# Seven-product form for the q, k and v projections of layer 2 and the q projection of layer 3 in a four-layer attention stack, with MLP weight sums made by tile pairs

## Chip, cores, metric

One core of a Trainium2 chip runs the whole program. The metric is the device time of one execution in microseconds (us); lower is better. Engines: PE (TensorE: matmuls into PSUM), PEld (its weight loads), DVE (VectorE), ACT (ScalarE), POOL (GpSimd), SP (SyncE, which issues the DMAs).

## What is computed

Four layers in a chain on x of shape (4 batches, 512 tokens, 512 features), all in float32, with a context of (4, 64, 512). Cut to what the change touches:

```python
# layer 0: two cross-attentions over the context, then gelu(h @ w_fc1 + b) @ w_fc2 + b, F = 2048
# layer 1: cross-attention with weights that are folded into the context
# layer 2, 16 heads of 32; keys and values from the 64 context rows AND from the 512 rows of x
q  = x @ q_w + q_b                                  # (512 x 512) @ (512 x 512) for each batch
kv = concat([ctx, x]) @ kv_w + kv_b                 # k and v, each 512 x 512 for each batch
x  = gelu(rmsnorm(softmax(q k^T) v @ out_w + out_b + x) @ mlp_w1 + b1) @ mlp_w2 + b2 + x
# layer 3, 16 heads; keys and values from the context alone
q  = layer_norm(x) @ q_w + q_b
x  = x + softmax(q k_ctx^T) v_ctx @ cproj_w + cproj_b
x  = x + gelu(layer_norm(x) @ fc_w + fc_b) @ proj_w + proj_b
```

## The kernel before

**Layout.** After layer 0's attention the activations lie transposed: `xT[b][c]` is a tile of 128 features by 512 tokens, four (c) for each batch b. A projection of one batch is thus 4 output tiles, each 4 matmuls of 128x128 weights by 128x512 tokens summed in a PSUM bank (`mm4`, L634). `projected` (L1140) does it for layer 3's q, `sliced` (L1148) for layer 2's q and k with weights loaded as slices of 128 columns, and for v the roles are swapped: x is the stationary side and `L2_wv` the moving one (L1246 to L1253). Each result leaves PSUM with a bias added (L493 on DVE, L496 and L492 on ACT, L1252 on DVE for v).

**MLP.** `mlp` (L910) already takes two batches at once by Strassen's scheme in Winograd's form: a 2x2 block product made with 7 block products instead of 8. The blocks are halves of the features by halves of the output columns on the weight side, and halves of the features by the two batches on the other. `stationary_sums` (L868) loads one quarter of a weight matrix (512 x 512) as four blocks of 256 KB and makes four sums of 128x512 elements; `moving_sums` (L886) makes eight sums for the two batches; `seven` (L899, its matmuls are L907) makes the products, 2 matmuls of 512 columns each. The sums of weights and activations go through `added` (L864), whose one instruction (L866) may run on DVE or on POOL.

**Order of the work.** Nothing is issued in the order in which it is written. `Plan` records every operation with an estimated cost for each engine it may run on, then `order` simulates the five engines and writes out one fixed sequence for each engine's queue. The highest-ranked ready operation on an engine goes first; it may run ahead of the oldest unfinished one by `AHEAD` = 150 us of PE work (loads: 60 us), and only if its buffers fit. SBUF is one arena of 24 blocks of 2080 floats in each partition, given out in halves of halves (a 512-float tile takes 520, a quarter block). Work that is further ahead than 15 us has to leave 4 whole blocks free. Where an attempt finds no room, `order` starts again with the look-ahead cut to 20 us around that place. PSUM is 8 banks.

**Streams.** The rank comes from `beside` (L275): several streams are interleaved by the share of their PE work that is done, so that MLP matmuls fill the waits of an attention. In time: layer 0's attention; MLP 0 of batches 0 and 1 beside layer 1's weights; MLP 0 of batches 2, 3 beside layers 1 and 2's attention of batches 0, 1; MLP 2 of 0, 1 beside layers 1 and 2's attention of 2, 3; MLP 2 of 2, 3 beside layer 3's attention of 0, 1; MLP 3 of 0, 1 beside layer 3's attention of 2, 3; MLP 3 of 2, 3 alone.

**Layer 2's attention** (`l2_attention`, L1239) then takes four heads at a time: scores of context (L1265) and of x (L1294, four matmuls on 32 rows each), maximum on DVE (L1305, L1307), exponential on ACT (L1317), transposes of the weights on PE (L1351, L1357), copies out (L487 on ACT, L488 on DVE), the product with v (L1381). Layer 3's scores are L1164, 4 matmuls of 256 columns at a time, its layer norms use L1182 to L1229.

Of the kernel before, what the change touches and what calls it, by code (L numbers as in the profile page):

```python
# [76 lines left out]
class View:  # L77
# [5 lines left out]
    def __init__(self, buf, key=None, path=()):  # L83
        self.buf, self.key, self.path = buf, key, path
# [112 lines left out]
class Plan:  # L197
# [8 lines left out]
    SHARED_DVE, SHARED_POOL = 0.45, 0.15  # L206
    PATIENCE = 3.0

    def __init__(self, sbuf, ahead, ahead_load, reserve):
        self.reserve = reserve  # L210
        self.sbuf = Memory(BLOCK, sbuf)
        self.psum = Memory(1024, 4)
        self.ahead, self.ahead_load = ahead, ahead_load
        self.ops = []
        self.pos = 0.0

    def sb(self, n):
# [56 lines left out]

    def beside(self, *streams):  # L275


        first, at = len(self.ops), self.pos
        spans = []
        for stream in streams:  # L280
            i, pos = len(self.ops), self.pos
            stream()
            length = max(self.pos - pos, 1e-9)
            spans += [((op.pos - pos) / length, op) for op in self.ops[i:]]
        spans.sort(key=lambda s: s[0])
        pos = at
        for i, (_, op) in enumerate(spans):
            op.n, op.pos = first + i, pos
            self.ops[first + i] = op
            pos += op.engines.get("PE", 0.0)  # L290

    def order(self):


        waits = [op.wait for op in self.ops]
        left = {id(b): (b, b.left) for op in self.ops for b in op.uses}
        narrow = []
        while True:
            for op, n in zip(self.ops, waits):
                op.wait = n  # L300
            for b, n in left.values():
                b.left, b.at = n, None
            self.sbuf.reset()
            self.psum.reset()
            out, at = self.attempt(narrow)
            if out:
                return out
            width = 100 + 100 * sum(lo <= at <= hi for lo, hi in narrow)
            if width > 1500:
                raise RuntimeError(f"no room at {at}: {self.sbuf.free}, {self.psum.free}")  # L310
            narrow.append((at - width, at + 50))
# [247 lines left out]
def stack(nc, const, sbuf, psum, a, out):  # L559
# [30 lines left out]
        mterm3.rearrange("p b s -> p (b s)"), mk_b, 0.0, LOWEST, ALU.is_equal, ALU.mult  # L590
    )

    pl = Plan(BLOCKS, AHEAD, AHEAD_LOAD, RESERVE)
    sb, ps = pl.sb, pl.ps

    def col(name, i=None):
# [4 lines left out]
    def pe(us):  # L601
        return pl.op(PE=us)
# [24 lines left out]
    def chunks(w):  # L627

        return w.rearrange("(c p) n -> p c n", p=P)
# [235 lines left out]
        with pl.op(DVE=t_dve(n), POOL=t_pool(n)) as o:  # L865
            o.tensor_tensor(out, x, y, op)  # L866

    def stationary_sums(src):  # L868

        a11, a12, a21, a22 = (  # L870
            loaded(chunks(src)[:, 2 * r : 2 * r + 2, m * 256 : m * 256 + 256], 2, 256).v(2, 256)
            for m in range(2)
            for r in range(2)
        )
        sums = [sb(512).v(2, 256) for _ in range(4)]
        added(sums[0], a21, a22, ALU.add, 512)
        added(sums[2], a11, a21, ALU.subtract, 512)
        added(sums[1], sums[0], a11, ALU.subtract, 512)
        added(sums[3], a12, sums[1], ALU.subtract, 512)

        def part(view):
            return lambda c, m: view[:, c, m * P : (m + 1) * P]

        return [part(v) for v in (a11, a12, a22, *sums)]

    def moving_sums(h0, h1):  # L886

# [8 lines left out]
            ops.append((b11, b21, b22, t4, t1, t2, t3))  # L896
        return [(lambda c, i=i: ops[c][i]) for i in range(7)]

    def seven(A, T, m):  # L899

        a11, a12, a22, s1, s2, s3, s4 = A
        b11, b21, b22, t4, t1, t2, t3 = T
        for lhs, rhs in ((a11, b11), (s2, t2), (s3, t3), (s1, t1), (a12, b21), (a22, t4), (s4, b22)):
            p = ps()
            with pe(2 * MM[512]) as o:
                for c in range(2):
                    o.matmul(p.v(), lhs(c, m), rhs(c), start=(c == 0), stop=(c == 1))  # L907
            yield p

    def mlp(layer, pair, hT, func, table, b1, b2):  # L910
# [21 lines left out]
            return t  # L932

        for q in range(F // 512):
            A = stationary_sums(a[f"L{layer}_w1"][:, q * 512 : (q + 1) * 512])
            g0, g1 = [None] * NC, [None] * NC

            def gelu(g, f, src):
                g[f] = sb(S)
                with act(S, table) as o:  # L940
                    o.activation(g[f].v(), src.v(), func, bias=col(b1, q * NC + f))  # L941

            for m in range(2):
                made = seven(A, T, m)
                u1 = moved(next(made))
                u2 = plus(next(made), u1)
                u3 = plus(next(made), u2)
                p5 = moved(next(made))
                gelu(g1, 2 + m, sum_of(p5, u3))
                u4 = sum_of(p5, u2)  # L950
                gelu(g0, m, plus(next(made), u1))
                gelu(g0, 2 + m, plus(next(made), u3))
                gelu(g1, m, plus(next(made), u4))
            A = stationary_sums(a[f"L{layer}_w2"][q * 512 : (q + 1) * 512, :])
            G = moving_sums(g0, g1)
            for m in range(2):
                made = seven(A, G, m)
                for r in kept[m]:
                    p = next(made)
                    if q == 0:  # L960
                        with either(S) as o:
                            o.move(r.v(), p.v())
                    else:
                        with dve(S) as o:
                            o.tensor_tensor(r.v(), p.v(), r.v(), ALU.add)  # L965
                for r, d in ((x0[m], m), (x0[2 + m], 2 + m), (x1[m], m)):
                    p = next(made)
                    with dve(S) as o:
                        if q == 0:
                            o.scalar_tensor_tensor(r.v(), p.v(), col(b2, d), r.v(), ALU.add, ALU.add)  # L970
                        else:
                            o.tensor_tensor(r.v(), p.v(), r.v(), ALU.add)
                if q == last:
                    p1, p6, p7, p5 = (r.v() for r in kept[m])
                    x11, x21, x12, x22 = x0[m].v(), x0[2 + m].v(), x1[m].v(), x1[2 + m].v()
                    added(x11, x11, p1, ALU.add, S)
                    added(p6, p6, p1, ALU.add, S)
                    added(p7, p7, p6, ALU.add, S)
                    added(x21, x21, p7, ALU.add, S)
                    added(p6, p6, p5, ALU.add, S)  # L980
                    added(x12, x12, p6, ALU.add, S)
                    added(p7, p7, p5, ALU.add, S)
                    with pl.op(DVE=t_dve(S)) as o:
                        o.scalar_tensor_tensor(x22, p7, col(b2, 2 + m), x22, ALU.add, ALU.add)
# [160 lines left out]
            o.shift(t.v(), p.v(), col(name, d))  # L1145
        return t

    def sliced(name, src, bias, d):  # L1148

        p = ps()  # L1150
        w = loaded(chunks(a[name][:, d * P : (d + 1) * P]), NC, P)
        with pe(4 * MM[512]) as o:
            mm4(o, p.v(), lambda c: w.v(NC, P)[:, c, :], lambda c: src[c].v())
        t = sb(S)
        with either(S) as o:
            o.shift(t.v(), p.v(), col(bias, d))
        return t

    def context_scores(q, kd, t, mterm, b, qs):

# [73 lines left out]

    def l2_context():
        row = load_row("L2_v_b")
        shared2.update(row=row, ckT=context_keys(2, "L2_k_b"), cv=context_values(2, row))

    def l2_attention(b):  # L1239
        qs = 1.0 / DH  # L1240
        row, ckT, cv = shared2["row"], shared2["ckT"], shared2["cv"][b]
        xb = xT[b]
        kd = diagonal_keys(ckT, b)
        wv = loaded(chunks(a["L2_wv"]), NC, 512)
        v = []
        for t in range(NT):  # L1246
            p = ps()
            with pe(4 * MM[512]) as o:
                mm4(o, p.v(), lambda c: xb[c][:, t * P : (t + 1) * P], lambda c: wv.v(NC, 512)[:, c, :])
            n = sb(D)  # L1250
            with dve(D) as o:
                o.tensor_tensor(n.v(), p.v(), row.v(), ALU.add)  # L1252
            v.append(n)  # L1253
        oT = []
        for g in range(NC):
            q = sliced("L2_wq", xb, "L2_xattn_q_b", g)
            k = sliced("L2_wk", xb, "L2_k_b", g)

            sc, mc = [], []
            for i in range(NT // 2):  # L1260
# [23 lines left out]
            for half in range(2):  # L1284
# [102 lines left out]
                            )  # L1387
                with dve(2 * P) as o:
                    o.tensor_tensor(made[:, half * 2 * P : (half + 1) * 2 * P].k(half), p[:, : 2 * P], rT.v(), ALU.mult)
            oT.append(made)  # L1390
        wo = loaded(chunks(a["L2_wo"]), NC, 512)
        y = []
        for d in range(NC):
# [17 lines left out]

    def l3_context():
        row = load_row("L3_xattn_v_b")
        shared3.update(ckT=context_keys(3, "L3_xattn_k_b"), cv=context_values(3, row))

    def l3_attention(b):
# [1 line left out]
        cv = shared3["cv"][b]  # L1418
        h = layer_norm(xT[b], "L3_xattn_ln1_w", "L3_xattn_ln1_b")
        kd = diagonal_keys(shared3["ckT"], b)  # L1420
        wq = loaded(chunks(a["L3_wq"]), NC, 512)
        q = [projected(wq, h, "L3_xattn_q_b", d) for d in range(NC)]
        prT = [sb(4 * S) for _ in range(2)]
        for t in range(NT):
            sc = context_scores(q, kd, t, mterm3, b, qs)
# [129 lines left out]

BLOCK, BLOCKS = 8 * KW, 24
AHEAD, AHEAD_LOAD, RESERVE = 150.0, 60.0, 4


# [54 lines left out]
```

## Time and profile before

| what | value |
|---|---|
| median of 3 runs | 2855.93 us (2852.36 to 2856.58) |
| profiled execution | 2855.12 us, of which the span from first to last instruction is 2853.2 us |
| mean granted TensorE clock | 0.994 |
| PE busy in the span | 2772.7 us, 10540 instructions |
| DVE / ACT / POOL busy | 1817.4 / 814.2 / 916.0 us |
| DMA | 129.62 MB, mean 45 GB/s |

How to read it: a float32 matmul stands in the trace as two records of its line (1344 matmuls of `seven` are 2688 records), so counts of records are twice the matmuls; transposes have one record. A record of a PE group has a duration from entry to end, and the next one enters before it has ended, so the pace is read from the chain of waits or a timeline, not from the mean duration. "Idle before" is the time for which an engine had nothing running ahead of an instruction, and the name after it is what came last. The windows view gives busy microseconds of each engine in a stretch of the span.

### The profile page before, as it was taken

Reading aid. Unit: us, or ns where it says so; the run is one execution under the profiler, and the core shown is the slowest. Engines: PE = TensorE matmul, PEld = TensorE weight load, DVE = VectorE, ACT = ScalarE, POOL = GpSimd, SP = SyncE. Lnnn points to the kernel's source line nnn. Section 1 sums busy time; section 2 is a strip of 40 time slices with the busy share of each in tenths; the row PEclk is TensorE's granted clock in tenths of the full one; section 3 lists DMA queues with packets and bytes.
Section 4 is the critical chain, followed back from the end, with each engine's and each line's share of the span. In section 5 each row is a group of like instructions: output and inputs, shape, how many; then the busy total and the mean of one; then the engine's idle time right before and its main releaser. Section 6 shows DMA issues by size and latency. Waiting matters only on the chain. (4 is left out here: it accounts for less than half of the span.)

```text
span 2853.2 us, 29411 instructions
## 1 busy us (share of the span) xinstructions
PE 2772.7 (97%) x10540; PEld 1499.2 (53%) x10540; DVE 1817.4 (64%) x3102; ACT 814.2 (29%) x1471; POOL 916.0 (32%) x859
## 2 busy tenths in 40 slices
PE   8999999999999999998999999999999998999999
PEld 6676666666654444544555555444444444444444
DVE  5645656555745567756677577576775677567665
ACT  1210212102311114634362355245432323232211
POOL 2710216202521241212124112311543456344531
PEclk9999999999999999999999999999999999999999
DMA  5022020120102110010012001101101120111110
GB/s 163 30 60 67 26 67 23 56 63 1 60 30 77 60 44 19 27 45 30 23 38 71 8 25 44 59 27 41 45 30 44 45 74 15 44 45 60 59 45 30
DMA packets 131025, 129.62 MB, mean 45 GB/s; under 512 B 6800, under 2 KB 105744, under 8 KB 130880
## 3 DMA queue, kind: packets, MB, share of 16 engines
q1 hardware_dynamic: 130512, 127.43, 14.1%
q8 instruction: 84, 1.38, 0.2%
q14 instruction: 61, 0.50, 0.1%
q0 software_dynamic: 80, 0.16, 0.0%
q10 hardware_dynamic: 288, 0.15, 0.0%
HBM read 123.52 MB, written 4.19 MB: 45 GB/s over the span
## 5 line engine op out<-in xcount | busy, mean ns | idle before, releaser
L907 PE MATMUL banks<-arena 128*128 128x512 f32 x2688 | 1210.1, 596 | 19.5 <-DVE arena L866 6.7
L634 PE MATMUL banks<-arena 128*128 128x260 f32 (+3 forms) x2480 | 825.9, 486 | 2.7 <-ACT arena L496 1.1
L907 PEld LDWEIGHTS banks<-arena 128*128 128x128 f32 x2688 | 497.6, 190 | 615.4 <-issue 528.3
L866 POOL TENSOR_TENSOR arena<-arena 128x512 f32<-128x512 f32 x304 | 437.1, 1445 | 678.1 <-DVE arena L488 173.3
L634 PEld LDWEIGHTS banks<-arena 128*128 128x128 f32 x2480 | 454.6, 189 | 329.3 <-issue 287.2
L488 DVE COPY arena<-banks 128x512 f32<-128x512 f32 (+3 forms) x526 | 305.4, 586 | 180.9 <-PE banks L907 66.3
L487 ACT COPY arena<-banks 128x512 f32<-128x512 f32 (+2 forms) x366 | 190.8, 542 | 710.5 <-PE banks L907 191.1
L866 DVE TENSOR_TENSOR arena<-arena 128x512 f32<-128x512 f32 x308 | 302.7, 989 | 69.2 <-ACT arena L941 26.3
L941 ACT ACTIVATE arena<-arena,cols 128x512 f32<-128x512 f32 x192 | 137.8, 721 | 448.8 <-DVE arena L866 221.4
L926 DVE TENSOR_TENSOR arena<-banks,arena 128x512 f32<-128x512 f32 x240 | 163.9, 686 | 131.1 <-PE banks L907 120.7
L1317 ACT ACTIVATE arena<-banks,arena 128x512 f32<-128x512 f32 x256 | 174.5, 686 | 115.1 <-DVE arena L1307 47.2
L823 POOL TENSOR_TENSOR arena<-arena 128x512 f32<-128x512 f32 x64 | 72.0, 1125 | 397.1 <-DVE arena L820 355.9
L1305 DVE TENSOR_REDUCE arena<-banks 128x1 f32<-128x512 f32 x256 | 167.6, 680 | 12.2 <-PE banks L1294 11.4
L1351 PEld LDWEIGHTS banks<-ident,arena 128*128 128x128 f32 x1024 | 120.8, 146 | 84.7 <-ACT arena L1317 36.4
L634 PE MATMUL banks<-ctxT,arena 128*128 128x256 f32 x640 | 151.8, 388 | 9.5 <-DMA arena<-in_L_wk 7.8
L493 DVE TENSOR_SCALAR arena<-banks,cols 128x256 f32<-128x256 f32 (+1 forms) x101 | 57.8, 573 | 161.6 <-PE banks L634 155.1
L1351 PE MATMUL banks<-ident,arena 128*128 128x128 f32 x1024 | 141.0, 283 | 13.3 <-ACT arena L1317 11.7
L634 PEld LDWEIGHTS banks<-ctxT,arena 128*128 128x128 f32 x640 | 121.9, 193 | 42.6 <-issue 13.5
L965 DVE TENSOR_TENSOR arena<-banks,arena 128x512 f32<-128x512 f32 x144 | 98.2, 685 | 65.1 <-PE banks L907 65.0
L1328 POOL TENSOR_TENSOR arena<-arena 128x256 f32<-128x256 f32 x64 | 40.2, 628 | 259.6 <-DVE arena L1307 183.6
L666 POOL TENSOR_SCALAR arena<-arena 128x512 f32<-128x512 f32 x48 | 99.8, 2086 | 31.3 <-DVE arena L661 13.6
L842 DVE TENSOR_TENSOR arena<-banks,arena 128x512 f32<-128x512 f32 x64 | 44.1, 690 | 94.5 <-PE banks L634 94.3
(141 smaller groups left out, 2308.2 us busy)
## 6 DMA issues: line engine op xcount, KB each, us to landing
arena<-in_L_w SPq DMA_DIRECT2D x192, 256.0 KB, 3.6
arena<-in_L_wk SPq DMA_DIRECT2D x48, 256.0 KB, 3.2
arena<-in_L_wqT SPq DMA_DIRECT2D x32, 256.0 KB, 4.0
arena<-in_L_wv SPq DMA_DIRECT2D x32, 256.0 KB, 3.6
arena<-in_L_wo SPq DMA_DIRECT2D x32, 256.0 KB, 3.4
arena<-in_L_wo SPq DMA_DIRECT2D x8, 1024.0 KB, 5.2
arena<-in_L_wv SPq DMA_DIRECT2D x6, 1024.0 KB, 7.0
arena<-in_L_wq SPq DMA_DIRECT2D x5, 1024.0 KB, 8.0
```

The source lines that it names most:

```text
L487: "ACT": lambda e, out, in_: e.copy(out, in_),
L488: "DVE": lambda e, out, in_: e.tensor_copy(out, in_),
L634: o.matmul(dst, lhs(c), rhs(c), start=(c == 0), stop=(c == NC - 1))
L666: o.tensor_scalar(n.v(), src[t].v(), mv.v(NT, 2)[:, t, 0:1], rstd[:, t : t + 1], ALU.subtract, ALU.mult)
L866: o.tensor_tensor(out, x, y, op)
L907: o.matmul(p.v(), lhs(c, m), rhs(c), start=(c == 0), stop=(c == 1))
L926: o.tensor_tensor(t.v(), p.v(), y.v(), ALU.add)
L941: o.activation(g[f].v(), src.v(), func, bias=col(b1, q * NC + f))
L965: o.tensor_tensor(r.v(), p.v(), r.v(), ALU.add)
L1305: o.tensor_reduce(m[:, i : i + 1].k(i), banks[i].v(), AX.X, ALU.max)
L1317: o.activation(y.v(), banks[i].v(), AF.Exp, bias=nm[:, i : i + 1].k(i), scale=qs, accum_out=sums[:, i : i + 1].k(i),)
L1351: o.transpose(p[:, c * P : (c + 1) * P], e[i][:, c * P : (c + 1) * P], ident)
```

## The change

Layer 2's q, k and v and layer 3's q now use the seven-product scheme inside one batch: the two halves of its 512 tokens stand where the MLP has two batches, so that a product has 256 moving columns instead of 512. `token_sums` makes eight sums of 128x256 from a batch's four tiles (once for q, k and v together in layer 2). For v, those are the stationary side and `value_sums` makes four sums of 128x512 of `L2_wv`. `seven_halves` writes two products into the two halves of a bank. `combined` puts the products together: four additions that read PSUM (three of 256 elements, one of 512, on DVE), two `added` of 256, and a first step (two halves by `either`, or for v one DVE addition of 512). The bias goes in with the first product for the first output tile, and the difference of the two tiles' biases (`bias_steps`) with a later one. Tiles come in pairs (m and m + 2), so layer 2 takes its head groups in the order 0, 2, 1, 3 and keeps q and k of a pair.

`stationary_sums` makes its sums for one pair of 128-column tiles at a time: two loads of 256 KB with rows of 512 bytes and four sums of 128x256, called once for each m, where it loaded four blocks with rows of 1 KB and made four sums of 128x512 for both.

`beside` only notes where each stream begins and ends. A new `merge`, called before ordering, interleaves them: of the streams whose next operation fits into `FULL` = 24 blocks of live buffers, the one with the smallest share of its PE work done goes next; if none fits, the one that takes least.

```diff
     def beside(self, *streams):
...
+            parts.append((i, len(self.ops)))
+        self.regions.append(parts)
+    def merge(self):
...
+                open_.sort(key=lambda k: gone[k] / total[k])
+                fit = [k for k in open_ if live + growth(ops[next_[k]]) <= self.full]
+                k = fit[0] if fit else min(open_, key=lambda k: growth(ops[next_[k]]))
...
-    def stationary_sums(src):
+    def stationary_sums(src, m):
+        t = sb(NC * 2 * P)
+        w = t.v(NC, 2, P)
+        for i in range(2):
+            load(w[:, :, i].k(i), chunks(src[:, (2 * i + m) * P : (2 * i + m + 1) * P]), NC * P)
...
+        added(s1, a21, a22, ALU.add, 2 * P)
+        added(s3, a11, a21, ALU.subtract, 2 * P)
+        added(s2, s1, a11, ALU.subtract, 2 * P)
+        added(s4, a12, s2, ALU.subtract, 2 * P)
...
+    def seven_halves(A, T):
+        a11, a12, a22, s1, s2, s3, s4 = A
+        b11, b21, b22, t4, t1, t2, t3 = T
+        for made in (((a11, b11), (s1, t1)), ((s2, t2), (s3, t3)), ((a12, b21),), ((s4, b22), (a22, t4))):
+            p = ps()
+            with pe(2 * len(made) * MM[256]) as o:
+                for i, (lhs, rhs) in enumerate(made):
+                    for c in range(2):
+                        o.matmul(p[:, i * 256 : (i + 1) * 256], lhs(c), rhs(c), start=(c == 0), stop=(c == 1))
+            yield p
+    def combined(made, first, third):
+        r = sb(2 * S)
+        mid = sb(512)
+        x = first(next(made))
+        p67 = next(made)
+        u2 = sb(256)
+        with dve(256) as o:
+            o.tensor_tensor(u2.v(), p67[:, :256], x[:, :256], ALU.add)
+        third(mid[:, 256:].k(1), p67[:, 256:], u2.v())
+        added(mid[:, :256].k(0), x[:, 256:], u2.v(), ALU.add, 256)
+        added(r[:, 768:].k(3), x[:, 256:], mid[:, 256:].k(1), ALU.add, 256)
+        p = next(made)
+        with dve(256) as o:
+            o.tensor_tensor(r[:, :256].k(0), p[:, :256], x[:, :256], ALU.add)
+        p = next(made)
+        with dve(512) as o:
+            o.tensor_tensor(r[:, 256:768].k(1), p.v(), mid.v(), ALU.add)
+        return r
...
     def l2_attention(b):
...
+        X = token_sums(xb)
+        W = value_sums(loaded(chunks(a["L2_wv"]), NC, 512))
...
+        for g in (0, 2, 1, 3):
+            if g < 2:
+                qs2 = projected_tiles("L2_wq", X, "L2_xattn_q_b", g)
+                ks2 = projected_tiles("L2_wk", X, "L2_k_b", g)
+            q, k = (r[:, :S] if g < 2 else r[:, S:] for r in (qs2, ks2))
...
     def l3_attention(b):
...
-        wq = loaded(chunks(a["L3_wq"]), NC, 512)
-        q = [projected(wq, h, "L3_xattn_q_b", d) for d in range(NC)]
+        X = token_sums(h)
+        q = [None] * NC
+        for m in range(2):
+            r = projected_tiles("L3_wq", X, "L3_xattn_q_b", m)
+            q[m], q[2 + m] = r[:, :S], r[:, S:]
```

## Prediction

> **What bounds the kernel now.** I read the page's busy shares first:
>
> ```profile
> span 2853.2 us, 29411 instructions
> PE 2772.7 (97%) x10540; PEld 1499.2 (53%) x10540; DVE 1817.4 (64%) x3102; ACT 814.2 (29%) x1471; POOL 916.0 (32%) x859
> PE   8999999999999999998999999999999998999999
> ```
>
> PE is busy for 97% of the span, so 80.5 us are idle in all. A stall can only win part of that; to go further the kernel needs less matmul time. Next, the windows view cut at the stages around the change (columns: PE, PEld, DVE, ACT, POOL busy, clock, DMA share, GB/s):
>
> ```profile
> 1050.00:1510.00 460.00, 437.14 (x2082) 223.87 (x2080) 302.50 (x653) 203.92 (x443) 97.28 (x117) 0.98 0.09 29
> 1510.00:1990.00 480.00, 461.90 (x2148) 235.34 (x2147) 318.22 (x636) 195.84 (x407) 112.95 (x128) 1.00 0.13 40
> 1990.00:2330.00 340.00, 333.18 (x1001) 156.66 (x1000) 237.74 (x319) 105.26 (x164) 154.85 (x119) 0.99 0.12 39
> 2330.00:2660.00 330.00, 318.10 (x849) 147.94 (x848) 227.47 (x265) 99.74 (x138) 163.49 (x120) 0.99 0.17 54
> ```
>
> The first two rows hold nearly all of layer 2's attention: 22.9 + 18.1 = 41.0 us idle in 940, DVE 620.7 us (66%), POOL 210.2 us (22%). The last two hold most of layer 3's: 6.8 + 11.9 = 18.7 us idle in 670, DVE 465.2 us (69%), POOL 318.3 us (48%). PE bounds both; DVE is next. The waits of PE, asked for 1000 to 2000 and for 2000 to 2700, name what ends the gaps:
>
> ```profile
> PE banks L1351 <- ACT arena L1317: 11.2, 8, 2.5
> PE banks L1294 <- ACT arena L1317: 9.9, 8, 2.3
> PE banks L907 <- ACT arena L1317: 5.8, 4, 2.7
> ```
>
> ```profile
> PE banks L907 <- DVE arena L866: 6.5, 3, 4.4
> PE banks L1217 <- POOL arena L1214: 6.3, 2, 3.4
> ```
>
> In layer 2 it is the softmax (DVE maximum, then ACT exponential) that is late; in layer 3 the sums and layer norms on DVE and POOL, at a change of stage. Last, the pace of a matmul, from runs in the chain of waits:
>
> ```profile
> 2227.55 10.30 PE banks L634 x24
> 2253.30 1.73 PE banks L1164 x8
> ```
>
> A record of 512 columns takes 10.30 / 24 = 0.429 us, one of 256 takes 1.73 / 8 = 0.216 us. A float32 matmul is two records.
>
> **What the Trainium skill says.** "TensorE: Matmul & The Clock Gate", "Step-by-step: what each phase is for": matmuls in a row are spaced by their moving columns, since the drain of one lies under the next. The trace agrees in shape: half the columns take 0.216 / 0.429 = 0.504 of the time. The same page, "LDWEIGHTS (loading the stationary operand)": a load's time goes with its columns, not with what it multiplies. Every load of 128x128 here takes about 190 ns whether 512 or 256 columns follow; so a product of 256 columns must hide the same load under half the time. It still does: L1164 loads before each record and keeps 216 ns. "GPSIMD Engine Reference", "Key points": POOL shares its SBUF interfaces with DVE instructions that read two SBUF operands. The additions at L866 show it: on DVE 627 ns at least, 693 median, 989 mean. "DMA: Bandwidth & Descriptors", "Specifications": pieces of at least 512 B go at line rate. The new rows are just 512 B; the trace has such loads (`L2_wq`, `L2_wk` slices, 256 KB): `L2_wq` lands after 2.8 us, against 3.6 us for the MLP's 1 KB rows.
>
> **1. Matmuls, on the path.** Sixteen projections change (q, k, v for four batches, q of layer 3 for four). Each had 16 matmuls of 512 columns, 32 x 0.429 = 13.73 us. Each will have 7 products x 2 feature chunks x 2 tile pairs = 28 matmuls of 256 columns, 56 x 0.216 = 12.11 us. That is 1.62 us saved each: **-26.0 us**, of which 12 x 1.62 = 19.5 in layer 2 and 6.5 in layer 3. PE's matmul records go from 10540 to 10540 - 512 + 896 = 10924. Bounds: the cheapest pace is the 0.216 above; the dearest in the trace is the group L634 with 256 columns on ctxT, 151.8 us / 640 = 0.237, which would leave 13.73 - 13.27 = 0.46 each, -7.4 us. I take 0.216, because L1164 runs between MLP matmuls as the new ones will and the ctxT group waits on loads at the start.
>
> **2. Vector work, beside PE.** Layer 2, per batch. Removed: 4 v additions (L1252, 0.69 us) and 8 exits with bias, mostly on DVE (L493 at 512 elements, 0.75 us, 28 records in the two layer-2 windows, so 7 per batch): 2.8 + 5.3 = 8.1 us of DVE. Added: six `combined`, each three PSUM additions of 256 (L1389: 0.424 us) and one of 512 (0.69) = 1.96, so 11.8; two first steps for v, 1.4; eight halves, of which I give DVE six at 0.45 = 2.7; then sums on either engine: 8 of tokens, 16 of weights and 12 in `combined` of 256 elements, 4 of 512 for v. For half of these DVE pays 18 x 0.42 + 2 x 0.69 = 8.9 us undisturbed and perhaps 13 with POOL beside it (the ratio 989 / 693), POOL 18 x 0.61 (L1328) + 2 x 1.28 = 13.5. Net about +19 us of DVE and +13.5 of POOL, four times: **DVE +76, POOL +54**. Layer 3 per batch, by the same prices: two `combined` 3.9, four halves half on DVE 0.9, twenty sums of 256 half on DVE 4.2 to 6.5, less half of four exits 1.5: +8.6, so **DVE +34, POOL +25** in all. DVE's load goes to about (621 + 76) / 920 = 76% from 66% in layer 2, and to about (465 + 34) / 664 = 75% from 69% in layer 3; POOL stays under 55%. None of this is on PE's queue, so it costs nothing by itself: MLP matmuls cover it. But the exponentials for which PE waits stand behind the maxima in DVE's queue, where the new additions now stand too. An estimate: PE's gaps grow with DVE's load, 41.0 x 76 / 66 - 41.0 = +6.2 and 18.7 x 75 / 69 - 18.7 = +1.6: **+8 us**. Bounds: -20 (a third of the 59.7 us of gaps goes, below) and +34 (rival B).
>
> **3. MLP sums by tile pairs.** 48 sets of 4 sums of 512 become 96 of 4 sums of 256. On DVE two at about 0.42 against 0.69 is +0.15 us each; if half of 192 run there, +14 us of DVE spread over some 2000 us. POOL is level (2 x 0.61 against 1.28). PE waits for L866 only at the stage changes (6.5 us above), where the first four sums are now half as long, which can win a microsecond or two. I take **0**, within -3 to +3.
>
> **4. Loads.** MLP: 4 of 256 KB per set before, 2 x 2 after; layer 2's q and k: 8 per batch before and after. Layer 3: one of 1 MB becomes four of 256 KB, 12 more issues on SP's queue, some 0.4 us each and nothing behind them that is late (nobody waited on `in_L_wq`). The DMA queue is at 14%. **0**. Were the cover gone, a load would show its 2.8 us at each first use.
>
> **5. Merging and room.** The page shows no arena room, so this is open in both directions. By the code, one weight set of an MLP quarter takes 2080 floats for one pair where it took 4160 for two, one to two blocks less with the next set in flight; token sums (8 x 260), value sums and kept q, k pairs take some 2.5 more. It roughly balances, so I take **0** apart from the bounds under 2.
>
> **Sum.** 2855.1 (profiled execution: span 2853.2 plus 1.9 around it) - 26.0 + 8 = 2837.1. The median of the runs is 0.8 above the profiled one: 2838.
>
> **Rivals.** *A, room is found:* smaller weight sets and the new merging let MLP matmuls reach the gaps. For it: the layer-2 gaps are short (at most 2.9 us) and MLP matmuls could fill them. Against: nothing shows that room held them back. At 10 us regained: 2855.1 - 26.0 - 10 + 0.8 = 2820. *B, DVE's queue decides (slower):* if delay grows like load / (1 - load), 0.66 gives 1.94 and 0.76 gives 3.17, so layer 2's gaps grow by 41.0 x 0.63 = 26, layer 3's by 18.7 x 0.35 = 7 (2.23 to 3.0): +33, 2863. It decides from 26 us of added gaps. For it: gaps end at L1317, which waits for L1307; against: the order is planned with DVE's costs in it, and MLP matmuls stand by. *C, the narrow products don't keep pace:* 0.237 each gives -7.4, with the +8 about 2856. For it: weight loads of 190 ns leave 26 ns of slack in 216; against: L1164.
>
> **Chances.** Forecast 0.48 (own range 2829 to 2847), A 0.25, C 0.14, B 0.13. A measurement of this kernel can tell about 0.2% (5.7 us) from no change. Faster: forecast and A, plus a third of C: 0.78. Same: the rest of C, 0.10. Slower: 0.12, nearly all B. The range leaves out A's last part, below 2812 (a third of the gaps regained is 2810), and B above 2860.
>
> **What would show it.** Right: 10924 PE records; runs of 56 new records in 12.1 us with 379 ns each; layer 2's stage shorter by about 13 us and layer 3's by about 5; PE idle near 88 us; DVE busy about 1940. A: idle under 75 us. B: idle above 106 us, on waits for L1317 and DVE. C: new runs slower than 0.22 us a record, PEld late. The prediction is wrong if the stage of layer 0 (before 780 us), which nothing touches, moves by more than a microsecond or two, or if gaps appear whose releaser is a load.

## The result and the profile after

The changed kernel takes 2809.78 us (median of 6 runs, 2808.83 to 2810.53), the kernel before on the same chip 2855.44 us: ratio 0.9842, 95% interval 0.9829 to 0.9854. That is 45.7 us less, where 17 were forecast. The profiled execution took 2809.43 us.

The busy shares of the changed kernel's page:

```profile
span 2807.7 us, 31089 instructions
PE 2741.5 (98%) x10924; PEld 1566.2 (56%) x10924; DVE 1905.9 (68%) x3344; ACT 825.1 (29%) x1503; POOL 1073.0 (38%) x1136
```

PE has the 10924 records that were counted ahead. It is busy for 31.2 us less, and idle for 66.2 us in place of 80.5: the gaps shrank by 14.3 us, where 8 more were forecast. DVE gained 88.5 us, POOL 157.

The same stretches as before, in the windows view (PE, PEld, DVE, ACT, POOL busy, clock, DMA share, GB/s):

```profile
1050.00:1510.00 460.00, 449.01 (x2344) 260.63 (x2343) 337.18 (x733) 213.00 (x456) 164.66 (x212) 1.00 0.13 40
1510.00:1990.00 480.00, 465.20 (x2407) 269.05 (x2407) 362.98 (x761) 214.71 (x462) 167.10 (x211) 1.00 0.10 30
1990.00:2330.00 340.00, 324.00 (x884) 158.19 (x883) 260.57 (x328) 101.93 (x142) 192.74 (x170) 0.97 0.16 46
2330.00:2660.00 330.00, 326.06 (x926) 161.46 (x925) 245.77 (x310) 94.80 (x135) 170.40 (x149) 1.00 0.17 51
```

In the two layer-2 stretches PE is idle for 11.0 + 14.8 = 25.8 us, not 41.0, although DVE's share rose from 66% to 74%. The clock column was 0.98 in the first of them and is 1.00 now. The gain lies in layer 2: its last score record started at 2019.4 us before (L1294) and starts at 1973.9 us now (L1447), 45.5 us earlier. From there to the end it is 833.8 us in both: layer 3's 6.5 us of matmul time do not show.

The waits of PE in the changed kernel, in 1000 to 2000 and in 2000 to 2700:

```profile
PE banks L1447 <- ACT arena L1470: 8.9, 9, 2.2
PE banks L1504 <- ACT arena L1470: 8.9, 11, 2.3
```

```profile
PE banks L963 <- DVE arena L982: 7.9, 5, 5.9
```

It is the same exponential for which PE waits in layer 2 (L1317 is L1470 now). In layer 3 the longest gap, 5.9 us, is again at the change of stage, behind an addition of the MLP on DVE. And the pace of the new matmuls, from the chain of waits:

```profile
2182.81 9.50 PE banks L1241 x44
```

9.50 / 44 = 0.216 us a record, as taken.

**A gap can cost more than its length.** What I had not priced is seen in the kernel before. Its timeline on PE (start, duration, records, and the idle time ahead in brackets):

```profile
1319.72 1.98 PE L907 MATMUL banks<-arena 128*128 128x512 f32 x4
1324.25 1.08 PE L1351 MATMUL banks<-ident,arena 128*128 128x128 f32 x4 [2.55 <-ACT arena L1317]
1326.03 2.09 PE L1294 MATMUL banks<-arena 32*128 32x512 f32 x8 [0.70 <-DVE arena L926]
1328.05 2.82 PE L1351 MATMUL banks<-ident,arena 128*128 128x128 f32 x12
```

and its windows view over the same time:

```profile
1320.00:1325.00 5.00, 2.45 (x8) 1.08 (x7) 5.00 (x10) 1.93 (x4) 3.37 (x3) 0.93 0.00 2
1325.00:1330.00 5.00, 4.30 (x19) 2.47 (x18) 3.73 (x8) 2.21 (x7) 0.61 (x1) 0.50 0.00 0
```

After a gap of 2.55 us the granted clock is 0.50. Eight score records (L1294) then take 2.09 us and twelve transposes (L1351) 2.82. At nearly the same place the changed kernel has a gap of 2.24 us with no slow stretch behind it, and the same groups take 1.14 and 1.53 us:

```profile
1321.49 1.14 PE L1447 MATMUL banks<-arena 32*128 32x512 f32 x8 [2.24 <-ACT arena L1470]
1322.57 1.53 PE L1504 MATMUL banks<-ident,arena 128*128 128x128 f32 x12
```

Between 1050 and 1990 us the kernel before has six gaps of 2 us or more on PE. The clock falls to half within some 3 us after five of them; the sixth, of 2.33 us, has nothing behind it. The changed kernel has two such gaps, of 2.24 and 2.31 us, and neither has. A gap of 2.20 us did bring half clock in another run (`qk_ahead` below), so what decides it isn't shown. In all, the clock stands at half for 23.9 of these 940 us before, and never after.

**The sum.** PE's busy time fell by 31.2 us. Of these, 26.0 are matmuls by count and pace. The other 5.2 are put down to the clock: the mean clock, which the profile gives to three decimals only, prices it at (1 - 0.994) x 2853.2 - (1 - 0.996) x 2807.7 = 17.1 - 11.2 = 5.9 us. With 14.3 us of gaps this makes up the span, 45.5 us shorter. Cut at the last score record of layer 2, which has all of layer 2's changed projections before it and all of layer 3's behind it, the change in us is:

| stretch | matmuls | gaps | rest of PE's busy time | sum |
|---|---|---|---|---|
| up to the last score record | -19.5 | -16.7 | -9.3 | -45.5 |
| from there to the end | -6.5 | +2.4 | +4.1 | 0.0 |

So layer 3's saving was made, and lost again. Part of the loss is at the change of stage. The longest gap behind that record, in the kernel before and then in the changed one:

```profile
2362.09 10.47 PE L907 MATMUL banks<-arena 128*128 128x512 f32 x20 [4.40 <-DVE arena L866]
2317.31 11.90 PE L963 MATMUL banks<-arena 128*128 128x512 f32 x20 [5.92 <-DVE arena L982]
```

The gap is 1.5 us longer, and the 20 records behind it (8.6 us at 0.429 each) take 1.4 us more than before. Why the order leaves a longer gap there is open.

### The profile page after: what moved, and what is told of

It reads as the page before. It is cut to its first block, busy times and chain, and to the rows that moved or that the text cites. A ratio compares the mean times of both kernels' runs of the same rounds, so it can differ in the third digit from the quotient of the medians.

```text
span 2807.7 us, 31089 instructions
## 1 busy us (share of the span) xinstructions
PE 2741.5 (98%) x10924; PEld 1566.2 (56%) x10924; DVE 1905.9 (68%) x3344; ACT 825.1 (29%) x1503; POOL 1073.0 (38%) x1136
## 5 line engine op out<-in xcount | busy, mean ns | idle before, releaser
L925 POOL TENSOR_TENSOR arena<-arena 128x256 f32<-128x256 f32 (+1 forms) x579 | 597.8, 1046 | 658.7 <-DVE arena L547 108.9
L963 PEld LDWEIGHTS banks<-arena 128*128 128x128 f32 x2688 | 499.0, 191 | 593.2 <-issue 503.7
L693 PE MATMUL banks<-arena 128*128 128x260 f32 (+3 forms) x1968 | 598.4, 459 | 3.0 <-ACT arena L555 1.1
L693 PEld LDWEIGHTS banks<-arena 128*128 128x128 f32 x1968 | 358.5, 189 | 212.4 <-issue 169.7
L546 ACT COPY arena<-banks 128x512 f32<-128x512 f32 (+3 forms) x403 | 209.8, 543 | 751.8 <-PE banks L963 218.2
L925 DVE TENSOR_TENSOR arena<-arena 128x256 f32<-128x256 f32 (+1 forms) x465 | 374.4, 819 | 49.4 <-ACT arena L998 19.1
L547 DVE COPY arena<-banks 128x512 f32<-128x512 f32 (+3 forms) x513 | 292.4, 576 | 157.8 <-PE banks L963 48.0
L982 DVE TENSOR_TENSOR arena<-banks,arena 128x512 f32<-128x512 f32 x240 | 164.7, 686 | 120.5 <-PE banks L963 108.6
L882 POOL TENSOR_TENSOR arena<-arena 128x512 f32<-128x512 f32 x64 | 71.8, 1122 | 388.5 <-DVE arena L879 348.9
L1241 PE MATMUL banks<-arena 128*128 128x256 f32 x896 | 206.3, 380 | 2.6 <-DVE arena L982 1.0
L1470 ACT ACTIVATE arena<-banks,arena 128x512 f32<-128x512 f32 x256 | 174.7, 687 | 82.0 <-DVE arena L1460 38.6
L1241 PEld LDWEIGHTS banks<-arena 128*128 128x128 f32 x896 | 168.6, 190 | 54.1 <-issue 21.6
L1021 DVE TENSOR_TENSOR arena<-banks,arena 128x512 f32<-128x512 f32 x144 | 98.4, 685 | 49.8 <-PE banks L963 49.4
```

Of the source, the lines that this page charges most:

```text
L546: "ACT": lambda e, out, in_: e.copy(out, in_),
L547: "DVE": lambda e, out, in_: e.tensor_copy(out, in_),
L693: o.matmul(dst, lhs(c), rhs(c), start=(c == 0), stop=(c == NC - 1))
L963: o.matmul(p.v(), lhs(c), rhs(c), start=(c == 0), stop=(c == 1))
L982: o.tensor_tensor(t.v(), p.v(), y.v(), ALU.add)
L1241: o.matmul(p[:, i * 256 : (i + 1) * 256], lhs(c), rhs(c), start=(c == 0), stop=(c == 1))
```

## Experiments

The question is whether the 20 us of gaps and slower PE time belong to the change, to which part of it, or to the one order that the planner happened to write.

**One part alone: weight sums by pairs** (`pairs_only`). The kernel before with the new `stationary_sums`, `seven` and `mlp`, all else old.

```diff
-            A = stationary_sums(a[f"L{layer}_w1"][:, q * 512 : (q + 1) * 512])
+            w1 = a[f"L{layer}_w1"][:, q * 512 : (q + 1) * 512]
...
-                made = seven(A, T, m)
+                made = seven(stationary_sums(w1, m), T)
```

The new merging needs no run of its own in these two kernels: put into the kernel before, or into this one, it leaves the same instructions in the same order on every engine. In the changed kernel it makes room: without it the ordering finds none for the seven-product form.

> The kernel before with only the MLP weight sums made by tile pairs; projections as they were, old interleaving. Theory 'pairs' (the 20 us beyond the matmul saving come from the MLP's smaller and earlier weight sums, which let MLP matmuls reach the gaps): 2835 to 2842, PE idle 60 to 66 us instead of 80.5. Rival 'projections' (the surplus comes with the seven-product projections themselves): 2852 to 2858, idle near 80 us. Rival 'order' (any change of the planner's order shifts the gaps by 10 us or more, either way): anything between 2840 and 2870, with the gaps at other places.

Measured: 2852.01 us, ratio 0.9985 (0.9979 to 0.9992), idle 79.6 us. At this order the pairs give 3.9 us against the kernel before, measured beside it (2855.88). That lies in the range of rival 'projections'; the pairs are not the main cause.

**Narrow matmuls alone** (`narrow`): each 512-column matmul of the sixteen projections as two halves of 256 columns (`mm8`), everything else in the order of `pairs_only`.

```diff
-            mm4(o, p.v(), lambda c: w.v(NC, P)[:, c, :], lambda c: src[c].v())
+            mm8(o, p, lambda c: w.v(NC, P)[:, c, :], lambda c: src[c].v())
```

> The kernel of the run with pairs alone, every instruction in the same order, but each 512-column matmul of layer 2's q, k, v and layer 3's q split into two of 256 columns with the same weights loaded for each: 256 matmuls become 512, and nothing is saved. It measures the pace of narrow matmuls alone. At 0.216 us a record the time is that of pairs alone within 2 us (1024 records, 0.003 us each more than half of 0.429: +1.5). At 0.237 a record (rival C of the prediction) it is 1024 x 0.0225 = 23 us longer.

Measured: 2854.62 us, ratio 0.9999 (0.9991 to 1.0008), 2.6 us above `pairs_only`, where +1.5, within 2, was expected at 0.216 and +23 at 0.237. The groups of this kernel show what was split:

```profile
L634 PE MATMUL banks<-arena 128*128 128x512 f32 x784 | 349.6, 593 | 0.9 <-DVE arena L923 0.7 <-DVE arena L488 0.2
L634 PE MATMUL banks<-arena 128*128 128x256 f32 x1056 | 238.8, 381 | 4.7 <-ACT arena L1231 3.0 <-DVE arena L967 1.7
```

1296 - 784 = 512 wide records became 1024 narrow ones (32 were there before). Rival C is out: at +2.6 us for 1024 records, the weight loads stay hidden.

**Layer 2 alone, layer 3 alone** (`l2_only`, `l3_only`): the changed kernel with the other layer's code as before. For layer 2 alone, and then for layer 3 alone:

```diff
-        X = token_sums(h)
...
+        wq = loaded(chunks(a["L3_wq"]), NC, 512)
+        q = [projected(wq, h, "L3_xattn_q_b", d) for d in range(NC)]
```

```diff
-                qs2 = projected_tiles("L2_wq", X, "L2_xattn_q_b", g)
-                ks2 = projected_tiles("L2_wk", X, "L2_k_b", g)
...
+            q = sliced("L2_wq", xb, "L2_xattn_q_b", g)
+            k = sliced("L2_wk", xb, "L2_k_b", g)
```

> The changed kernel with layer 3's q as before, so 12 of the 16 projections changed. By matmul time alone it lies 4 x 1.62 = 6.5 us above the changed kernel, 2816. Theory 'pairs': 2814 to 2819. Rival 'projections': the surplus goes with the projections, three quarters of it stays: 2819 to 2824. Rival 'order': off by 10 us or more from 2816.

> The changed kernel with layer 2's attention as before, so only layer 3's q (4 of 16 projections) changed, with the sums by tile pairs and the new merging. Theory 'pairs': pairs alone minus 6.5, 2829 to 2836. Rival 'projections': 2855 minus 6.5 minus a quarter of 20, 2842 to 2846. Rival 'order': off by 10 us or more from both.

Measured: 2803.19 us (ratio 0.9813, 0.9800 to 0.9827) and 2843.90 us (0.9957, 0.9945 to 0.9970). Against `pairs_only`, layer 3's q gives 8.1 us, close to its 6.5 of matmuls. Layer 2's gives 48.8, with 19.5 of matmuls. Both together give 42.2, less than layer 2 alone. Only theory 'order' allowed for such a result (layer 2 alone is 13 us off the 2816 of the matmuls); it didn't say which way.

**The look-ahead cut** (`full23`): `FULL = 23` in place of 24.

> The changed kernel with the merging's room limit at 23 blocks in place of 24; nothing else. With 24 the ordering finds no room late in layer 2 and layer 3 and cuts its look-ahead from 150 to 20 us of PE work over operations 4598 to 5448 of 8025; with 23 it never has to in layers 1 to 3. Theory 'room' (that cut is why layer 3's seven-product q makes the kernel 6.6 us slower than the run with layer 2 alone instead of 6.5 faster): 2794 to 2800, and the gaps around 2020 to 2060 and 2260 to 2320 us shrink. Rival 'vector' (layer 3's new additions on DVE and POOL at the stage change cost the 13 us): 2806 to 2813, gaps as they are.

Measured: 2806.43 us (0.9828, 0.9813 to 0.9843), 3.4 us below the changed kernel, with intervals that overlap. Theory 'room' falls: with the full look-ahead back, layer 3's saving is still missing. The time lies in the range of rival 'vector', which this run doesn't test further.

**Another order of the same instructions** (`ahead140`, `ahead160`, `l2ahead140`, `l2ahead160`, `after140`, `after160`, `before140`, `before160`): one number changed.

```diff
-AHEAD, AHEAD_LOAD, RESERVE = 150.0, 60.0, 4
+AHEAD, AHEAD_LOAD, RESERVE = 140.0, 60.0, 4
```

> The run with pairs alone, with the planner's look-ahead at 140 us in place of 150: the same instructions in another order. It measures how much the order alone moves the time. Theories 'pairs', 'ahead' and 'load': within 4 us of 2852. Rival 'order': off by 10 us or more.

> The run with layer 2 alone, with the look-ahead at 140 us: the other side of the same test. If the 48 us that layer 2's seven-product form saved are its own: within 5 us of 2803. Rival 'order' (29 of them are a lucky order): it falls back toward 2832, by 10 us or more.

> The changed kernel with the planner's look-ahead at 140 us in place of 150. Theory 'order' (the matmul saving is 26 us and the rest of the 45.7 was the luck of one order): back toward 2829, 2820 to 2840. If the surplus belongs to the change: 2805 to 2815.

> The run with pairs alone with the look-ahead at 160 us, a third order of the same instructions without the seven-product projections. Theory 'order' expects 2845 to 2865, another place than 2852 and 2860 (what 150 and 140 gave).

> The changed kernel with the look-ahead at 160 us: its third order. Against the run with pairs alone at 160 (2867.7) the matmul saving alone gives 2842. Theory 'order' (surplus all luck): about 2842. Theory 'both' (the change shortens gaps and half-speed clock by itself, by 10 us or so, and the order adds its own spread on top): 2825 to 2836.

> The kernel before with the look-ahead at 160 us. Gives the spread of the kernel before's own order, and the part of pairs alone at 160 (2867.7). Theory 'order': 2850 to 2875, not within 3 us of 2856. If the sums by pairs do nothing by themselves: near 2868.

> The changed kernel with layer 3's q as before, look-ahead 160 us. At 150 it was 6.6 us below the changed kernel, at 140 it was 10 above, where matmul time alone puts it 6.5 above. Theory 'order': the difference from the changed kernel at 160 again falls anywhere within 15 us of +6.5.

> The kernel before with the look-ahead at 140 us, its third order. If the weight sums by pairs do nothing by themselves: within 8 us of pairs alone at 140 (2859.8), as at 150 (3.9 apart) and 160 (6.4 apart). The change at 140 is then this minus 2823.4; a shift that stays (45.7 at 150, 40.1 at 160): 2860 to 2872.

**q and k two head groups ahead, plain projections** (`qk_ahead`, and `qk140`, `qk160` at the other look-aheads): the kernel of `pairs_only` in which the matmuls stay as they were, but q and k come in the pairs of the changed kernel.

```diff
...
-        for g in range(NC):
-            q = sliced("L2_wq", xb, "L2_xattn_q_b", g)
-            k = sliced("L2_wk", xb, "L2_k_b", g)
+        for g in (0, 2, 1, 3):
+            if g < 2:
+                for i in (g, g + 2):
+                    qk[i] = [sliced("L2_wq", xb, "L2_xattn_q_b", i)]
+                for i in (g, g + 2):
+                    qk[i].append(sliced("L2_wk", xb, "L2_k_b", i))
+            q, k = qk[g]
```

> The run with pairs alone, but with plain projections of layer 2's q and k made for two head groups at once, in the order of the changed kernel (q and k of groups 0 and 2, then those two groups' softmax, then 1 and 3). No matmul is saved. Theory 'ahead' (the seven-product form shortens the gaps because it delivers q and k of two groups before either is needed, so that the scores can run further ahead): layer 2's gaps and half-speed clock shrink as they did in the run with layer 2 alone, total 2822 to 2835. Rival 'load' (the gaps shrink because PE has 19.5 us less work and the vector engines more time per matmul, or by another effect of the seven products themselves): no change, 2849 to 2855. Rival 'order': off by 10 us either way without a change of the gaps at the exponentials.

> Plain projections with layer 2's q and k made two head groups ahead, look-ahead 160 us. If making them ahead shortens the gaps by itself: 15 us or more below pairs alone at 160 (2867.7), 2840 to 2853. If the 17 us at 150 were luck: 2860 to 2875.

> Plain projections with layer 2's q and k made two head groups ahead, look-ahead 140 us. At 150 and 160 this lay 17.0 and 27.5 us below pairs alone. If that is the placing of q and k and not luck, it is 10 us or more below pairs alone at 140 (2859.8): 2832 to 2850. If luck: 2850 to 2870.

All orders together, medians in us (the kernel before at 150 was measured beside each group of runs, with medians from 2855.4 to 2856.3; 2855.8 stands for them):

| kernel | look-ahead 140 | 150 | 160 | mean |
|---|---|---|---|---|
| before | 2876.2 | 2855.8 | 2874.1 | 2868.7 |
| pairs alone | 2859.8 | 2852.0 | 2867.7 | 2859.8 |
| pairs, q and k ahead, no seven products | 2851.7 | 2835.1 | 2840.2 | 2842.3 |
| changed, but layer 3's q as before | 2833.4 | 2803.2 | 2828.8 | 2821.8 |
| changed | 2823.4 | 2809.8 | 2834.0 | 2822.4 |

Down a column, the change gives 52.8, 46.0 and 40.1 us. Along a row, order alone moves the time by 16 to 30 us, and single executions of one kernel lie up to 12 us apart (`qk140`). So single comparisons of a few us between these kernels tell little. Three runs fell outside what was expected: `qk140` is 8.1 us below pairs alone, not 10 or more, and so in the range put down to luck; `ahead160` is above its range of 2845 to 2865; `before140` is 16.4 us from pairs alone, not within 8. `ahead140`, 7.8 us from pairs alone, lies between its two ranges. `after140` lies in the range of 'order' and `after160` in that of 'both', so these totals alone don't decide between luck and a saving that stays.

In the totals, pairs alone gives 16.4, 3.8 and 6.4 us (mean 8.9), q and k ahead with no matmul saved another 8.1, 17.0 and 27.5 (mean 17.5), and the changed kernel is 36.4, 42.2 and 33.7 below pairs alone (mean 37.4), each time more than its 26.0 of matmuls.

**What the order moves, and what it doesn't.** The traces show more than the totals. The next table has the start of the last score record of layer 2 (us), and in brackets how long PE is idle between 1050 and 1990 us:

| kernel | 140 | 150 | 160 |
|---|---|---|---|
| before | 2034.5 (38.2) | 2019.4 (41.0) | 2038.2 (38.1) |
| pairs alone | 2026.8 (34.7) | 2009.1 (37.6) | 2021.1 (33.8) |
| pairs, q and k ahead, no seven products | 2014.1 (25.9) | 1992.5 (26.5) | 2007.9 (25.4) |
| changed, but layer 3's q as before | 1983.5 (25.1) | 1970.0 (25.0) | 1989.3 (26.9) |
| changed | 1988.8 (25.6) | 1973.9 (25.8) | 1995.1 (29.1) |

Up to this record the change is worth 45.7, 45.5 and 43.1 us: what it gives in layer 2 does not hang on the order. q and k ahead alone bring the idle time from 34 to 38 us down to 25 to 27, in each order. The seven products add vector work in that stretch (DVE busy for 700 us in place of 634, both at 150) and leave the idle time where it was at 140 and 150; at 160 it is 3.7 us more. They start the record 25.3, 18.6 and 12.8 us earlier, in the mean 18.9, close to their 19.5 us of matmuls.

The order moves the rest. In the first 780 us, which no edit here touches, PE is idle for 10.4 to 10.9 us in all five kernels at 150 and for 18.1 to 18.7 us at 140 and 160. The stretch behind the last score record takes 831 to 845 us, in no order of the kernels. There layer 3's 6.5 us come and go: 838.5 us before and 832.9 changed at 140, 833.8 and 833.8 at 150, 836.0 and 836.3 at 160. In the totals, the changed kernel less the one with layer 3's q as before is -10.0, +6.6 and +5.2 us, in the mean nothing.

The busy shares on the pages of pairs alone and of q and k ahead, both at 150:

```profile
PE 2769.2 (97%) x10540; PEld 1494.9 (52%) x10540; DVE 1829.8 (64%) x3186; ACT 819.3 (29%) x1477; POOL 925.4 (32%) x962
```

```profile
PE 2764.0 (98%) x10540; PEld 1496.1 (53%) x10540; DVE 1821.3 (64%) x3166; ACT 799.6 (28%) x1462; POOL 954.5 (34%) x984
```

and the cores view of the two (span and mean granted clock), in the same order:

```profile
core 0: 2848.8 us, clock 0.995
```

```profile
core 0: 2830.3 us, clock 0.998
```

The same 10540 records, 13.3 us less idle (79.6 to 66.3), of which 11.1 lie in the layer-2 stretch of the table, and 5.2 us less busy, at a clock of 0.998. Between 1050 and 1990 us the clock stands at half for 17.1 us in pairs alone and for 3.4 with q and k ahead.

**What the vector work costs, with the order held** (`hollow`, `double`). Both keep the changed kernel's plan; only what a new sum does is altered (`token_sums`, `value_sums`, and `stationary_sums` of the q and k weights use `summed` in place of `added`). `double` makes each sum twice; `hollow` leaves the sum out and puts a fill with zeros and an addition of two columns in its place. The edit of `double`:

```diff
+    def summed(out, x, y, op, n):
+        with pl.op(DVE=t_dve(n), POOL=t_pool(n)) as o:
+            o.tensor_tensor(out, x, y, op)
+            o.tensor_tensor(out, x, y, op)
```

> The changed kernel with the same order of instructions on every engine, but the new sums for the projections (of tokens, of L2_wv and of the q and k weights) left out: each is a fill with zeros and an addition of two columns, on the engine where the sum ran. So the products are wrong and the vector load is lighter, with nothing moved. If the prediction's step 2 is right (new additions lengthen PE's gaps by some us, bound +33): 2798 to 2806. If the additions are fully hidden: 2807 to 2811. If DVE's queue decides (rival B at full size): 2775 to 2790.

> The changed kernel with the same order, but each of those new sums made twice in a row on the same engine, some 160 more additions of 256 elements and 16 of 512 (about 40 to 60 us more on DVE and on POOL). Hidden: 2808 to 2814. By gaps in proportion to DVE's load (66 us of idle x 0.04): +3, 2813. By load / (1 - load): +15 or more, 2825 and up.

Measured: `hollow` 2805.53 us (0.9823, 0.9808 to 0.9838), 4.3 below the changed kernel, with intervals that overlap; `double` 2872.32 us (1.0056, 1.0041 to 1.0071), 62.5 above it. Both fall in a range in which the additions cost something: `hollow` in that of step 2, just, and `double` in that of load / (1 - load). The page and the two largest waits of PE in `double`:

```profile
PE 2759.4 (96%) x10924; PEld 1569.5 (55%) x10924; DVE 1973.0 (69%) x3427; ACT 824.0 (29%) x1503; POOL 1150.3 (40%) x1229
```

```profile
PE banks L968 <- DVE arena L987: 12.1, 11, 6.2
PE banks L1509 <- ACT arena L1475: 8.8, 11, 2.3
```

67 us more on DVE and 77 on POOL cost 62.5 us: idle rose from 66.2 to 108.7, and PE's busy time by 17.9 with the same matmuls. Here vector work that the order hasn't planned for is hardly hidden, though DVE is at 69%. `hollow` took off only 14.7 us of DVE and 35.4 of POOL: on DVE a fill (272 ns) and its small addition (318) are not much shorter than the sum that they replace (707 in the mean). So its 4.3 us bound nothing from above. A plan that knows of the doubled sums was not tried.

## Why the prediction was wrong, by its own steps

**Step 1, matmuls, right.** 10924 records, 0.216 us each; `narrow` shows some 2.6 us of cost for the narrow form over 1024 records. -26.0 stands. One reading was too wide: not every 128x128 load takes 190 ns. Those of the transposes take 141 to 146 in the mean; those of the new products do take 186 to 192.

**Step 2, vector work: the price half right, the effect wrong.** DVE gained 88.5 us against about 124 (76 + 34 + 14), POOL 157 against 79: more sums went to POOL than half, and each was dearer. At 256 elements L925 takes 707 ns on DVE and 798 on POOL in the mean, against the 420 to 600 and 610 used. The step then let PE's gaps grow with DVE's load, by 8 us. They fell by 14.3. The rule was an argument from averages. In layer 2, DVE's load of 700 us in place of 634 came with the same gaps (25.8 and 26.5 us at 150; at 160 it was 3.7 us more), so work that the plan knows costs PE little there; `double` shows that unplanned work can cost a lot. Rival B, which asked for more than 106 us of idle time, is out: there are 66.2.

**Step 3, sums by pairs at 0: small but not nothing.** 3.9 us at this order, 16.4 and 6.4 at the others. In the layer-2 stretch the idle time is 3.4 to 4.3 us shorter in each order. What in them does it isn't shown.

**Step 4, loads at 0: right.** No gap of note ends on a load but the one at the start, 7.3 us for 7.8 before. The reading that rows of 512 bytes land sooner (2.8 us against 3.6) doesn't hold throughout: in the changed kernel the same kind of load takes 3.2 us for the MLP and 3.8 for the q weights.

**Step 5, room and order at 0: with the +8 of step 2, this is what failed.** I treated the order of the work as unchanged apart from room. The seven-product form delivers q and k of two head groups at a time. That alone, with plain matmuls, took 17.0 us off at this order and 8.1 and 27.5 at the others, and brought layer 2's gaps to where the changed kernel has them. The prediction also had no term for PE's pace outside the changed matmuls: its busy time fell by 5.2 us more than theirs, which goes with the half-speed stretches that vanish from layer 2.

**Rival A** had the right sign and a smaller size (10 us). Of its means, the smaller weight sets have a share (step 3); whether room does, no run shows; the main one, q and k ahead, it didn't name. Its far end, 2810 with 20 us of gaps regained, is the measured time only by chance: 14.3 us were regained, and 5.2 us of PE's pace happen to fill the rest. The sign set for a false prediction, a shift of layer 0's stage, did not come: PE is idle there for 10.8 us before and 10.4 after.

**Layer 3** saved its matmul time, and lost it to a longer gap and slower matmuls behind the last score record. At the other look-aheads that stretch is 5.6 us shorter than before (140) and 0.3 longer (160), while it scatters by 14 us over all kernels and orders. A cut look-ahead is excluded as the reason by `full23`; why the order does so is open.

**What can be said of the 45.7 us:** 26.0 are matmuls (shown by count and pace), 14.3 are gaps (shown by the page), and some 5 are PE time at a higher clock (argued from the granted clock; no run changed the clock alone). The gaps close in layer 2, at all three look-aheads, and q and k ahead is the part that closes most of them. It was shown on plain projections; inside the changed kernel it can't be taken out, since there the tiles are made in pairs. In the totals, 26.0 + 17.5 = 43.5 us is more than the mean of 37.4 below pairs alone. The 6 us between are about what layer 3's q should have saved and in the mean did not: for the kernel without it, 19.5 + 17.5 = 37.0 stands against a mean of 38.0. How much of the last few us is the luck of one order stays open.

## What to carry to other kernels

Where one engine is at 97%, count its work for the floor of a change, but don't hold the gaps fixed: an edit that makes results available earlier lets a planner fill gaps that have nothing to do with the work saved. With a planned static order, run each version at two or three settings of the planner before reading a difference of a per cent; here order alone was worth up to 30 us. And compare the traces at a point with the same work on both sides: up to the last score record of layer 2 the three orders agreed on the change within 3 us, where the totals differed by 13. When pricing a gap on PE, look at the pace of the work behind it too.

## What was not expected of the hardware

A gap of 2.55 us on PE was followed by a stretch at a granted clock of 0.50, in which twelve transposes took 0.235 us each (2.82 / 12) in place of 0.128 (1.53 / 12); gaps of 2.24 and 2.33 us had no such stretch behind them. Matmuls of 256 columns, each with its own 190 ns weight load, keep half the time of 512 columns over hundreds of records (0.216 and 0.429 us). And in the kernel before, the additions of L866 on DVE took 692 ns in the mean where no POOL tensor instruction ran beside them (106 of 308), and 1381 ns where one ran nearly all the while (55).
